# The forward transform of a graph layer's convolution, on two halves of TensorE's rows

## The chip, the cores and the metric

The kernel runs on one core of a Trainium2 chip, in float32. The metric is the time of one launch on the device in microseconds (us); smaller is better.

## What is computed

For 32 graphs of 512 nodes with 256 channels: a layer norm and a relu give `h`; then a layer with a convolution branch, a message branch and a gated update (GRU) is added to `x`. The part that the change touches is in the convolution branch:

```python
h = relu(layernorm(x))
xc = transpose(h, (0, 2, 1))
t = relu(bn1(conv1d(xc, conv1_w, pad=0)))       # 256 -> 256 channels, 1 tap
t = bn2(conv1d(t, conv2_w, pad=8))              # 256 -> 256 channels, 17 taps
x_conv = transpose(relu(t + xc), (0, 2, 1))
# message branch: A = exp(-dist(s, s)) * adj;  x_nmp = A @ relu(h @ w_msg.T + b_msg)
# GRU of [x_conv, x_nmp] and h;  out = x + GRU
```

## The kernel before

The convolution with 17 taps is done in frequencies. The 512 tokens of an image are cut into `W` = 8 pieces of `V` = 64 tokens; each piece, padded to `L` = 80, is transformed by a product with a constant matrix (`fwd`) of 64 rows and 80 columns. The frequencies are multiplied with the transformed weights (`product`, tile py), and brought back later (`inverse`, L585).

The images run in two groups of `GB` = 16. For each group `first_part` goes through the images in a written order (`tc.manual_schedule`): for image b the statistics of image b+2 (VectorE), the transpose of image b+1 (`transpose_h`, tile phT, TensorE, then VectorE into hT), the normalisation of b+2 (VectorE, tile xn), `conv1(b)` (16 records of TensorE in tile pc, then an addition on VectorE and a relu on ScalarE into h), and `windows_to_freq(b - 1, xf)`, the step that is changed. The order of the last calls is: `conv1` of the last image, the transform of the image before it, `by_chunks` (ScalarE copies into hq), the transform of the last image, `by_chunks` of the group's first image. The next step, `message` (tile pm), reads hq.

Between these steps other work is put in through `between(b)`. In the first group it is `weights_to_freq` (L256, tile pw): four products of 17 rows each, on rows 0, 32, 64 and 96, into four banks, which ScalarE and VectorE copy to wst. One such step comes before the transform and one or two after it. In the second group it is `combine_weights` (L886): three loads of GRU weights on the queue of SP, one after the other, and additions on GpSimd and copies on ScalarE, in the same queues as the square root for the layer norm (rstd, L291) and the loads of x.

`windows_to_freq` takes H1, the h of one image, as a tile of 128 tokens by 4 chunks by 256 channels. A chunk holds two pieces of 64 tokens. Before, one product handles both pieces at once: the stationary operand is 128 tokens by 128 channels, and `fwd` is block diagonal, 128 rows by 160 columns, so half of it is zeros. Two chunks go into one bank (320 columns used), and ScalarE copies the bank into xf, whose order is channel, frequency, window. An image takes 2 channel halves x 2 banks x 2 chunks = 8 products and 4 copies.

All banks of PSUM (8) come from one pool, `bank(name)`, and are used in turn; an instruction that needs a bank waits for the reader of the one that had it before. In the profile a float32 product leaves two weight loads and two matmul records; a transpose leaves one.

## Time and profile before

| | |
|---|---|
| median of 8 runs | 1845.65 us (1843.18 to 1849.98) |
| the profiled execution: its own time | 1847.65 us |
| the profiled execution: span from first to last instruction | 1845.9 us |
| mean granted TensorE clock | 0.996 |
| TensorE busy | 1824.3 us (99%) |
| VectorE / ScalarE / GpSimd busy | 1106.7 / 582.4 / 588.4 us |
| first group, first part (30 to 160 us): TensorE busy 130.0 of 130 us, DMA share | 0.93 |
| second group, first part (480 to 578 us): TensorE busy 96.52 of 98 us, DMA share | 0.67 |
| tile px: matmul records, busy, median of one | 512, 77.5 us, 299 ns |
| tile px: weight loads, median of one | 512, 190 ns |
| tile px: copies by ScalarE, median of one | 128, 439 ns |

How to read it: matmul records overlap, so the time of one (299 ns) is longer than the distance to the next. For what a block costs, take the distance from its first start to the first start of the block behind it, in the timeline. PEld is the loading of stationary operands, PE the products.

### The profile page before, as it was taken

To read this page: it belongs to the slowest core of one execution; us is meant where nothing else is said; L and a number is where in the kernel's file an instruction comes from. 1 tells how busy PE (TensorE), PEld (TensorE's weight loads), DVE (VectorE), ACT (ScalarE), POOL (GpSimd) and SP (SyncE) were. 2 spreads that over 40 slices of the span, in tenths; PEclk is the share of its full clock that TensorE was granted. 3 is DMA by queue.
4 is the path that set the end of the run, shared out by engine and by line. 5 is a ranking of instruction groups with operands and counts; after the bars stand their busy time and mean duration, and the time that the engine had idled before them with its cause. 6 is when DMAs were issued, how large, how long until landed. Compare 5 with 4: busy or idle time off the path is not lost.

```text
span 1845.9 us, 20105 instructions
## 1 busy us (share of the span) xinstructions
PE 1824.3 (99%) x6610; PEld 1088.5 (59%) x6610; DVE 1106.7 (60%) x2220; ACT 582.4 (32%) x1083; POOL 588.4 (32%) x572
## 2 busy tenths in 40 slices
PE   8999999999999999999999999999999999999998
PEld 6777666666988676665545554555455544555443
DVE  6774656554885545545266466655666466645666
ACT  4545444432345333333222221222122221222121
POOL 3331333334432344444421323133222323133221
PEclk9999999999999999999999999999999999999999
DMA  8999888775678887777421443234422442244412
GB/s 226 303 278 240 225 240 241 214 188 182 210 245 207 240 248 232 220 203 257 121 86 35 120 120 104 55 81 120 120 81 40 120 120 90 51 99 120 113 24 52
DMA packets 307452, 289.26 MB, mean 157 GB/s; under 512 B 148028, under 2 KB 237148, under 8 KB 306964
## 3 DMA queue, kind: packets, MB, share of 16 engines
q1 hardware_dynamic: 281300, 224.22, 45.8%
q10 hardware_dynamic: 19024, 38.68, 5.9%
q0 software_dynamic: 7024, 25.07, 4.8%
q8 instruction: 53, 0.87, 0.2%
q14 instruction: 51, 0.42, 0.1%
HBM read 191.50 MB, written 96.40 MB: 156 GB/s over the span
## 4 chain that ended last, share of the span: by engine, by line
PE 88%; DMA 4%; DVE 3%; issue 2%; POOL 1%; ACT 1%; SPq 0%; POOLq 0%; ACTq 0%; DVEq 0%
PE pg L597 29%; PE pn L597 14%; PE pn L489 11%; PE py L393 10%; PE pm L439 6%; PE pc L585 5%; PE pc L328 4%; PE px L343 3%; PE pw L256 2%; PE pd L474 2%; DMA w<-in_w_ihT_dram 1%; PE phT L312 1%; DMA hT<-hd 1%; DMA yd<-y 1%; PE psr L463 1%
## 5 line engine op out<-in xcount | busy, mean ns | idle before, releaser
L489 PE MATMUL pn<-A,msg 128*128 128x512 f32 x512 | 225.6, 593 | 0.8 <-DVE A L480 0.8
L597 PE MATMUL pg<-hp,sw 128*128 128x512 f32 x434 | 221.8, 593 | 0.7 <-DVE rz L616 0.5
L597 PE MATMUL pg<-np,sw 128*128 128x512 f32 x434 | 221.6, 592 | 0.0
L597 PE MATMUL pg<-cp,sw 128*128 128x512 f32 x434 | 221.6, 592 | 0.0
L575 POOL TENSOR_TENSOR hp<-hp 128x512 f32<-128x512 f32 x64 | 81.3, 1280 | 412.3 <-DMA hp<-hd 263.6
L372 POOL TENSOR_TENSOR both<-xf 128x256 f32<-128x256 f32 x78 | 60.4, 774 | 322.8 <-PE py L393 291.2
L489 PEld LDWEIGHTS pn<-A,msg 128*128 128x128 f32 x512 | 96.9, 190 | 110.9 <-issue 105.6
L575 POOL TENSOR_TENSOR cp<-cp 128x512 f32<-128x512 f32 x64 | 80.4, 1267 | 230.0 <-ACT cp L591 228.8
L393 PE MATMUL py<-wt,both 128*128 128x256 f32 x624 | 150.5, 384 | 0.7 <-issue 0.7
L612 ACT ACTIVATE rz<-rz,brz 128x512 f32<-128x512 f32 x93 | 67.0, 721 | 260.2 <-DVE rz L616 260.2
L400 DVE TENSOR_TENSOR y<-y,py 128x256 f32<-128x256 f32 x78 | 31.8, 408 | 189.8 <-ACT y L399 189.8
L597 PEld LDWEIGHTS pg<-hp,sw 128*128 128x128 f32 x434 | 82.2, 190 | 104.7 <-issue 97.8
L597 PEld LDWEIGHTS pg<-np,sw 128*128 128x128 f32 x434 | 82.5, 190 | 103.8 <-issue 103.8
L597 PEld LDWEIGHTS pg<-cp,sw 128*128 128x128 f32 x434 | 82.5, 190 | 103.8 <-issue 103.8
L393 PEld LDWEIGHTS py<-wt,both 128*128 128x128 f32 x624 | 114.1, 190 | 43.1 <-issue 27.6
L480 DVE TENSOR_TENSOR A<-e,at 128x512 f32<-128x512 f32 x128 | 114.8, 935 | 37.4 <-ACT e L477 37.2
L359 POOL TENSOR_TENSOR wsum<-wt 128x512 f32<-128x512 f32 x78 | 108.8, 1396 | 55.1 <-DMA wt<-wd 46.2
L735 ACT ACTIVATE nt<-nt,vech 128x512 f32<-128x512 f32 x64 | 46.2, 722 | 235.8 <-DVE nt L734 235.8
L328 PE MATMUL pc<-w,hT 128*128 128x256 f32 x512 | 118.3, 385 | 2.0 <-DVE hT L316 2.0
L439 PE MATMUL pm<-wmsg,hq 128*128 128x259 f32 x512 | 117.4, 382 | 0.2 <-ACT sl L460 0.2
L597 PE MATMUL pn<-cp,sw 128*128 128x512 f32 x224 | 114.4, 592 | 0.0
L597 PE MATMUL pn<-np,sw 128*128 128x512 f32 x224 | 114.4, 592 | 0.0
(146 smaller groups left out, 2959.6 us busy)
## 6 DMA issues: line engine op xcount, KB each, us to landing
wt<-wd SPq DMA_DIRECT2D x160, 256.0 KB, 4.2
adj<-in_adj_dram SPq DMA_DIRECT2D x128, 256.0 KB, 5.3
wd<-wst SPq DMA_DIRECT2D x64, 320.0 KB, 5.4
yd<-y ACTq DMA_DIRECT2D x80, 256.0 KB, 4.0
yt<-yd SPq DMA_DIRECT2D x30, 640.0 KB, 7.3
hd<-hT SPq DMA_DIRECT2D x32, 512.0 KB, 4.4
nd<-nmp ACTq DMA_DIRECT2D x32, 512.0 KB, 4.1
xb<-in_x_dram SPq DMA_DIRECT2D x128, 128.0 KB, 3.7
```

The costliest lines, as they stand in the source:

```text
L328: nc.tensor.matmul(p[:, j, :], HT[b][:, ic, c * P : (c + 1) * P], w1[:, ic, :], start=(ic == 0), stop=(ic == DC - 1))
L343: nc.tensor.matmul(p[:, j * 2 * L : (j + 1) * 2 * L], H1[b][:, c0 + j, ic * P : (ic + 1) * P], fwd, start=True, stop=True)
L359: nc.gpsimd.tensor_tensor(t, WT[g, u][:, 0], WT[g, u][:, 1], op=ALU.add)
L372: nc.gpsimd.tensor_tensor(both[:, 0], re, im, op=ALU.add)
L393: nc.tensor.matmul(dst, v[:, ic, :], w[:, ic, :], start=(ic == 0), stop=(ic == DC - 1))
L439: nc.tensor.matmul(p[:, : D + NS], hq[:, ic, c * P : (c + 1) * P], wmsg[:, ic, :], start=(ic == 0), stop=(ic == DC - 1))
L480: nc.vector.tensor_mul(A[b][:, mc, :], e, at)
L489: nc.tensor.matmul(p, MSG[b][:, mc, dc * P : (dc + 1) * P], A[b][:, mc, :], start=(mc == 0), stop=(mc == NC - 1))
L575: nc.gpsimd.tensor_tensor(t[:, dst, :], t[:, a, :], t[:, b, :], op=sub)
L585: nc.tensor.matmul(bk[:, t0:t1], YT[p][j][:, c, oc * P : (oc + 1) * P], back[:, n : n + t1 - t0], start=(c == 0), stop=(c == len(spans) - ...
L597: nc.tensor.matmul(bk[:, t], sw[:, k, q, o, :], terms[k][q][:, t], start=(first and i == 0), stop=(i == len(ks) - 1), skip_group_check=True)
L612: nc.scalar.activation(rz[:, g, j, :], src, AF.Sigmoid, bias=brz[:, g : g + 1], scale=1.0)
```

## The change

One product per piece instead of one per chunk. `fwd` becomes 128 rows by 80 columns, the same 64 rows of the matrix twice. A chunk's even piece (tokens 0 to 63) is multiplied by rows 0 to 63 of `fwd`, its odd piece (tokens 64 to 127) by rows 64 to 127, each with a stationary operand of 64 rows and 128 columns. Even pieces go into one bank, odd ones into another; a bank takes all four chunks of an image (320 columns used). The products alternate between the two banks. ScalarE copies the two banks after all eight products of a channel half, each to every second window of xf. An image now takes 2 channel halves x 4 chunks x 2 pieces = 16 products and, as before, 4 copies of 320 columns.

```diff
-    forward = np.zeros((2 * V, 2 * L))
-    forward[:V, :L] = forward[V:, L:] = spectrum[:V]
+    forward = np.concatenate([spectrum[:V]] * 2)
...
-    fwd = early.tile([P, 2 * L], FP, name="fwd")
+    fwd = early.tile([P, L], FP, name="fwd")
...
     def windows_to_freq(b, xf):
         w0 = (b % GB) * W
-        per = 2
         for ic in range(DC):
-            for c0 in range(0, NC, per):
-                p = bank(f"px_{b}_{ic}_{c0}")
-                for j in range(per):
-                    nc.tensor.matmul(p[:, j * 2 * L : (j + 1) * 2 * L], H1[b][:, c0 + j, ic * P : (ic + 1) * P],
-                                     fwd, start=True, stop=True)
-                w = w0 + 2 * c0
-                nc.scalar.copy(xf[:, ic, :, w : w + 2 * per],
-                               p[:, : per * 2 * L].rearrange("p (w f) -> p f w", f=L))
+
+            ps = [bank(f"px_{b}_{ic}_{k}") for k in range(2)]
+            for c in range(NC):
+                for k, p in enumerate(ps):
+                    rows = slice(V * k, V * (k + 1))
+                    nc.tensor.matmul(p[:, c * L : (c + 1) * L], H1[b][rows, c, ic * P : (ic + 1) * P],
+                                     fwd[rows, :], start=True, stop=True)
+            for k, p in enumerate(ps):
+                nc.scalar.copy(xf[:, ic, :, w0 + k : w0 + W : 2],
+                               p[:, : NC * L].rearrange("p (w f) -> p f w", f=L))
         del H1[b]
```

## The prediction

> **What bounds the kernel now.** First the page's busy shares, then the groups of TensorE by shape, for the size of what is changed:

> ```profile
> PE 1824.3 (99%) x6610; PEld 1088.5 (59%) x6610; DVE 1106.7 (60%) x2220; ACT 582.4 (32%) x1083; POOL 588.4 (32%) x572
> ```

> ```profile
> L343 PE MATMUL px<-fwd,h 128*128 128x160 f32 x512 | 77.5, 306 | 0.0
> ```

> TensorE is busy all the time, and the step that is changed (tile px) has 77.5 us of it: 32 calls of `windows_to_freq`, each 16 records (a float32 product leaves two, so 8 products). A busy TensorE may still be standing in a queue, though, so next I read the blocks of TensorE in order of time, in the two stages that hold these calls. A middle image of the first group:

> ```profile
> 106.05 2.44 PE L343 MATMUL px<-fwd,h 128*128 128x160 f32 x16
> 108.42 1.88 PE L256 MATMUL pw<-w2p,taps 17*80 17x512 f32 x8
> 110.23 1.09 PE L312 MATMUL phT<-ident,xn 128*128 128x128 f32 x8
> 111.16 3.62 PE L328 MATMUL pc<-w,hT 128*128 128x256 f32 x16
> 114.71 1.10 PE L256 MATMUL pw<-w2p,taps 17*80 17x512 f32 x8
> ```

> Start to next start, the first pw block after a pc takes 1.03 us (114.71 to px at 115.74), but the pw block after px takes 1.81 (108.42 to 110.23). The other engines show why:

> ```profile
> 107.64 1.53 ACT L266 COPY wst<-pw 80x512 f32<-80x512 f32 x3
> 109.22 0.21 PEld L256 LDWEIGHTS pw<-w2p,taps 17*80 17x80 f32 x2 [0.27 <-ACT wst L266]
> 109.58 1.44 DVE L264 COPY wst<-pw 80x512 f32<-80x512 f32 x2 [1.93 <-PE pw L256]
> ```

> The pw block behind px waits for banks that ScalarE empties, and ScalarE started on them late, after the relu of h, which follows VectorE's adds, which follow VectorE's statistics, which follow VectorE's copies of the last pw. That ring (VectorE copies, statistics, hT, xn, h; ScalarE h, copies of pw; the pw block; VectorE copies) does not contain px. In twelve middle images the excess of the pw block is 0.18 to 0.84 us, 0.58 on average. In the second group there is no pw; there I read blocks and then the chain that ended last:

> ```profile
> 532.54 2.34 PE L343 MATMUL px<-fwd,h 128*128 128x160 f32 x16
> 534.71 1.04 PE L312 MATMUL phT<-ident,xn 128*128 128x128 f32 x8
> 535.59 3.62 PE L328 MATMUL pc<-w,hT 128*128 128x256 f32 x16
> 539.04 2.34 PE L343 MATMUL px<-fwd,h 128*128 128x160 f32 x16
> ...
> 545.54 2.34 PE L343 MATMUL px<-fwd,h 128*128 128x160 f32 x16
> 549.29 1.72 PE L312 MATMUL phT<-ident,xn 128*128 128x128 f32 x8 [1.41 <-DVE xn L304]
> ```

> ```profile
> 482.95 7.06 DMA w<-in_w_hhT_dram
> ...
> 507.49 9.29 DMA w<-in_w_ihT_dram
> ...
> 536.72 8.34 DMA w<-in_w_ihT_dram
> ```

> From 480 to 549 us the chain runs through three weight loads for `combine_weights`, GpSimd's additions behind them and VectorE's steps, not through TensorE, which stands still 1.41 us at 549.29 for it. Only after that are TensorE's blocks the chain.

> **The change part by part.** *The products.* Before, a px call lasts 2.17 us start to start (532.54 to 534.71), so a record of 160 columns costs 2.17/16 = 0.136. After, a call has 32 records of 80 columns, 16 on each half of the rows. Do halves run side by side, and what limits one half? The trace has no 64-row product; the nearest row is pd, four products on rows 0, 32, 64 and 96:

> ```profile
> 311.00 0.31 PEld L474 LDWEIGHTS pd<-sr,sl 9*128 9x128 f32 x8 [0.34 <-issue]
> ```

> Eight weight loads of 128 columns, 0.183 each by the tile's view, fill 0.31 us: four begin together, and the next four about 0.11 later. So loads on different rows overlap, and one set of rows takes one load per 0.107 (0.31 less 0.183, less the 0.02 in which the four begin). Streaming 80 columns costs less: records of 512 and 256 columns come every 0.43 (pn, last stage) and 0.216 (3.45/16 in pc), so 0.83 ns a column, 0.07 for 80. The load is the limit: 16 rounds of 0.108, the last without a following load: 15 x 0.108 + 0.08 = 1.70. A call saves 2.17 - 1.70 = 0.47. Bounds: streaming alone would limit (16 x 0.07 = 1.1, saving 1.07), or loads of both halves in series (32 x 0.107 + 0.07 = 3.49, costing 1.32). I take 1.70, since pd is the closest row.

> *Going over to half rows and back.* The trace has this between 128 rows and 17 or 9 rows. A pc block lasts 3.55 before pw (111.16 to 114.71) but 3.45 before px: 0.09 to enter. The pw block's two rounds of 0.43 make 0.86 of its 1.03; about 0.07 of the rest is its first, smaller load, 0.10 leaving. px between pw and pw lasts 2.37, not 2.17: 0.09 for the next entry, 0.11 for first weights that nothing hides. phT behind pw takes 0.93, not 0.87: 0.06. So half-row px costs, from pc and into phT, 0.09 + 0.11 + 0.10 + 0.06 = 0.36, into pc or pm 0.41; bounds 0, if halves need no such step, and about double. In the second group a call therefore nets 0.47 - 0.36 = 0.11. In the first group most px calls already stand between two pw, and the step is paid now. [...]

> *Copies.* Four per call as before, each 128x320 (434 to 442 ns); two now come free together after each half of the call. Their output steps by two elements instead of running over four neighbours; no row shows that for ScalarE. A copy at half the speed would still end before phT needs its bank in the first group (the first px copy ends about 0.65 us before the phT block), and ScalarE sits idle for 52.9 us waiting for h in the second; I take 0, bound 2.5 us (eight copies ahead of hq, 0.3 each). *The constant* fwd halves in size and loads at the start under w1: 0.

> *What arrives at the end.* First group: the first call is followed by 1.6 us of waiting: 0. Twelve middle calls are outside the ring: 0 (bound 0.47 each, 5.6). The call at 154.28, whose pw blocks wait for nothing now: 0.47 less some waiting for px copies, 0.3. The two joint calls at 162.09 (4.35 to pm): 31 x 0.108 + 0.08 + 0.41 = 3.84, saving 0.51; but pm reads hq, which ScalarE copies until then:

> ```profile
> 164.81 1.17 ACT L425 COPY hq<-hT 128x512 f32<-128x512 f32 x2
> ```

> so pm can't start before some 166.03 instead of 166.44: 0.41. Second group: eleven calls up to 549: 0, the loads set the end (bound 0.11 each). Calls at 554.39 and 560.90: 0.11 each; at 567.40, into pc: 0.06; the joint calls at 573.03 by the same limit (hq until 576.92): 0.40. Sum: 0.3 + 0.41 + 0.22 + 0.06 + 0.40 = 1.4 us. The profiled execution took 1847.65 with a span of 1845.9, 2.0 over the median of 1845.65. So its own time would be 1846.3, and the median 1844.2.

> **The rivals.** *The loads of the two halves go in series* (slower). A block of 128 tokens then takes 4 x 0.107 = 0.43 instead of 0.27, a call 1.32 more. First group: twelve calls with 0.58 of cover, (1.32 - 0.58) x 12 = 9; the last three calls 3 x 1.32 + 0.41 = 4.4. Second group: eleven x 1.68 less about 2 of present waits = 16.5; afterwards 3 x 1.68 + 3.05 = 8. Together 38: 1883.7. It decides from about 0.27 us a block on: there the steps between row modes alone (14 x 0.36 + 0.41 - 2) make 3.5 us. Against it: the eight pd loads in 0.31 us. For it: no product of 64 rows was seen, and none kept two halves going over 16 rounds.

> *The waits follow TensorE after all* (faster): the ring and the load chain begin earlier because TensorE does. Then 12 x 0.47 + 11 x 0.11 = 6.8 more, 1837.4. For it: VectorE waits 1.93 us for the pw block, so the ring has a TensorE part. Against it: that part waits for ScalarE.

> **How the numbers follow.** A measurement of this kernel can tell about 0.2%, 3.7 us, from no change. My forecast, 1844.2, has 0.56 (own range 1841 to 1848); 0.50 of it within 0.2%, 0.04 faster, 0.02 slower. The faster rival has 0.24, 0.20 of it past the line; serial or partly serial loads 0.20, 0.18 past it. Faster 0.24, same 0.56, slower 0.20. The range takes in the faster rival and loads that overlap in part, and leaves out full series: 1837.4 to 1852.

> **What would show it.** px: 1024 records; a lone call of the second group 1.70 + 0.11 + 0.10 = 1.9 us from px start to phT start, and the pc before it 3.55 instead of 3.45; a middle image of the first group with px at 1.9 too and a pw block behind it longer by what px lost; that image's period unchanged (9.57 us from phT at 110.23 to phT at 119.80 now). The stillness at 549 us grows or starts sooner. Wrong it would be if px calls take over 2.2 us (series), or if the first group's period shrinks by 0.4.

## The result and the profile after

The kernel after takes 1853.59 us (median of 15 runs, 1849.13 to 1862.66), the kernel before 1846.28 beside it (42 runs): ratio 1.0038, 95% interval 1.0029 to 1.0047. The change costs some 7 us, where 1.4 us less were forecast; the measured median also lies above the range. Two causes make up the loss: in the first group the granted clock of TensorE falls (0.95 from 35 to 165 us in the profile, before 1.00), because a half-row call uses half as many cells of the array (1.07 us of the whole array instead of 2.13, an estimate below); in the second, a call issues twice the instructions (32 records instead of 16), and fetches of TensorE's code fall into the two weight loads that set the end (10.41 and 8.72 us, before 9.29 and 8.34).

The parts of the change did what was said of them. First the page's busy shares, then the group of px by shape:

```profile
PE 1826.4 (99%) x7122; PEld 1083.1 (59%) x7122; DVE 1108.5 (60%) x2220; ACT 582.4 (32%) x1083; POOL 589.1 (32%) x572
```

```profile
L343 PE MATMUL px<-fwd,h 64*128 64x80 f32 x1024 | 66.8, 277 | 0.5 <-DVE h L330 0.5
```

512 records more, 10.7 us less of px than the 77.5 before, and yet TensorE as a whole is busy 2.1 us longer. What else got longer stands in the timeline of TensorE, over two middle images of the first group (start, length, records):

```profile
105.29 1.43 PE L343 MATMUL px<-fwd,h 64*128 64x80 f32 x18
106.87 1.11 PE L343 MATMUL px<-fwd,h 64*128 64x80 f32 x14 [0.15 <-DVE h L330]
107.92 2.13 PE L255 MATMUL pw<-w2p,taps 17*80 17x512 f32 x8
109.98 1.72 PE L311 MATMUL phT<-ident,xn 128*128 128x128 f32 x8
111.50 4.71 PE L327 MATMUL pc<-w,hT 128*128 128x256 f32 x16
116.14 1.10 PE L255 MATMUL pw<-w2p,taps 17*80 17x512 f32 x8
117.17 2.02 PE L343 MATMUL px<-fwd,h 64*128 64x80 f32 x32
119.12 1.10 PE L255 MATMUL pw<-w2p,taps 17*80 17x512 f32 x8
120.15 1.09 PE L311 MATMUL phT<-ident,xn 128*128 128x128 f32 x8
```

The pc block, untouched by the change, takes 4.64 us to the next start (111.50 to 116.14) where it took 3.55; phT takes 1.51 instead of 0.93. The granted clock says why. In the windows view (from and to, length, then busy time with records of TensorE, weight loads, VectorE, ScalarE and GpSimd, then the granted clock, the share of the DMA engines and GB/s), first before, then after:

```profile
35.00:165.00 130.00, 130.00 (x776) 94.23 (x775) 97.20 (x252) 69.97 (x157) 39.54 (x60) 1.00 0.93 281
```

```profile
35.00:165.00 130.00, 129.44 (x955) 92.09 (x954) 95.13 (x242) 67.01 (x149) 39.15 (x60) 0.95 0.89 267
...
106.90:110.30 3.40, 3.40 (x25) 1.98 (x26) 1.41 (x3) 3.40 (x9) 0.00 (x0) 1.00 0.89 293
110.30:113.70 3.40, 3.40 (x14) 2.95 (x12) 3.37 (x12) 0.89 (x2) 0.97 (x1) 0.50 0.91 266
```

For 3.4 us TensorE runs at half speed, after 3.4 us in which it was "busy" for all of 3.40. Over 35 to 165 us the clock is 0.95; before it was 1.00 there. The half-clock stretches of 3.4 us begin at 89.8, 110.3, 130.8 and 151.2 us, besides 6.8 us from 28.4 on; before had two up to 165 us, at 12.6 and 29.6, and none in the middle images. The page's own clock row shows 9 in every slice in both kernels, since a slice is 46 us. From the px at 84.73 to the px at 157.92 seven images take 73.19 us; before, from 85.94 to 154.28, 68.34.

The profiled execution of the kernel after (own time 1847.78 us) is the shortest of its sixteen, with a mean clock of 0.992; the others have 0.987 to 0.992 (median 0.991), those of before a median of 0.996. The longest, 1862.66, has 0.987. In the traces of before and after every stretch of the clock is at 1.00 or 0.50; if that holds in the other runs too, 0.996 is 15 us at half speed and 0.991 is 33 us, 18 us more, which is up to 9 us of TensorE's work (an estimate). Run by run the time follows the clock: a straight line through the 16 runs of the kernel after, and another through the 108 runs of before that were taken beside all experiments, both fall by 2.0 us for each 0.001 of clock. By that the 0.005 between the medians are some 10 us (an estimate), so the clock alone is large enough for the whole loss; what the code fetch adds to the time has to be read from pairs of kernels, below.

The second group, in the timeline and in the chain that ended last:

```profile
529.07 2.02 PE L343 MATMUL px<-fwd,h 64*128 64x80 f32 x32
531.02 1.10 PE L311 MATMUL phT<-ident,xn 128*128 128x128 f32 x8
...
551.12 1.72 PE L311 MATMUL phT<-ident,xn 128*128 128x128 f32 x8 [0.75 <-DVE xn L303]
```

```profile
507.75 10.41 DMA w<-in_w_ihT_dram
...
538.17 8.72 DMA w<-in_w_ihT_dram
```

A lone call is 1.945 us (529.07 to 531.02), as predicted. But the two loads on the chain, 9.29 and 8.34 us before, are 1.12 and 0.38 longer, and phT comes at 551.12 instead of 549.29 (the first px of this group began 0.24 us later than in before).

### The profile page after: what moved, and what is told of

The parts are those of the page before. It is cut to its first block, busy times and chain, and to the rows that moved or that the text cites. A ratio compares the mean times of both kernels' runs of the same rounds, so it can differ in the third digit from the quotient of the medians.

```text
span 1846.0 us, 21126 instructions
## 1 busy us (share of the span) xinstructions
PE 1826.4 (99%) x7122; PEld 1083.1 (59%) x7122; DVE 1108.5 (60%) x2220; ACT 582.4 (32%) x1083; POOL 589.1 (32%) x572
## 4 chain that ended last, share of the span: by engine, by line
PE 84%; DVE 2%; issue 2%; DMA 2%; POOL 1%; SPq 0%; ACT 0%; POOLq 0%; DVEq 0%; ACTq 0%
PE pg L597 29%; PE pn L597 14%; PE pn L489 12%; PE py L393 11%; PE pm L439 6%; PE pc L585 5%; PE pd L474 2%; PE pc L327 2%; DMA w<-in_w_ihT_dram 1%; PE px L343 1%; PE psr L463 1%; PE phT L311 1%; DVE stats L284 0%; DVE xn L303 0%; PE pw L255 0%
## 5 line engine op out<-in xcount | busy, mean ns | idle before, releaser
L597 PEld LDWEIGHTS pg<-hp,sw 128*128 128x128 f32 x434 | 82.2, 190 | 104.8 <-issue 97.1
L327 PE MATMUL pc<-w,hT 128*128 128x256 f32 x512 | 123.2, 396 | 1.6 <-DVE hT L315 1.6
L597 PE MATMUL pn<-hp,sw 128*128 128x512 f32 x224 | 114.4, 592 | 0.0
```

The source lines that it names most:

```text
L327: nc.tensor.matmul(p[:, j, :], HT[b][:, ic, c * P : (c + 1) * P], w1[:, ic, :], start=(ic == 0), stop=(ic == DC - 1))
L597: nc.tensor.matmul(bk[:, t], sw[:, k, q, o, :], terms[k][q][:, t], start=(first and i == 0), stop=(i == len(ks) - 1), skip_group_check=True)
```

## The experiments

The theory formed from the two profiles was that dips of the clock in the first group make the loss, by one of two reasons: too few cells of the array in use, or TensorE's waiting and the dearer steps between row modes. All ratios are to the kernel before, run beside it, with 95% intervals.

**Which group loses.** e1 and e2 keep both forms of the step and choose by the image:

```diff
+    def windows_to_freq(b, xf):
+        (by_halves if b >= GB else by_chunks_of_two)(b, xf)      # e1; e2: b < GB
```

> Half rows in the second group of images only, full rows in the first. The theory that I form from the two traces: what is lost is lost in the first group, where the granted clock falls to one half for stretches of 3.4 us (five times between 28 and 155 us after the change, three times in the whole launch before it, each costing about 1.7 us). It expects the first group's times of before, a mean clock of 0.995 to 0.997, and 1845 to 1846 us beside 1846.3 of before (1.1 us saved by the late calls of the second group). The rival, that going over to half rows costs more than I priced wherever it happens, expects about half of the loss here, 1849 to 1850.

> Half rows in the first group only, full rows in the second. The theory of the clock in the first group expects the whole loss, 1852 to 1855 us with a mean clock of 0.989 to 0.991. The rival of a dear step between row modes expects 1849 to 1850, since most calls of the first group stand between two pw and paid that step before the change.

e2: 1.0031 (1.0020 to 1.0041), median clock 0.992, half-clock stretches at the same places as in the kernel after. e1: 1.0020 (1.0008 to 1.0031), and this was the surprise: not a gain of 1 us, but a loss. Its first group was as before; in the second TensorE got ahead, stood still longer before the step at 549 (1.78 us before phT, 1.41 in before), and a stretch of half clock followed:

```profile
549.20:552.60 3.40, 1.55 (x15) 1.04 (x13) 2.08 (x5) 0.27 (x1) 3.01 (x4) 1.00 0.64 235
552.60:556.00 3.40, 3.40 (x12) 2.85 (x12) 3.37 (x13) 2.72 (x7) 0.27 (x1) 0.50 0.39 154
```

Its w_ihT loads took 10.67 and 8.85 us. With half rows in the first group alone (e2) the first load took 9.3. So both groups lose: the first by the clock, the second by longer loads, and by the clock too (one stretch, at 552.6 us in e1 and at 523.3 in the kernel after).

**What lowers the clock: cells or waiting?** Between the first and the last change of the clock in the traces of before and after, changes lie a whole multiple of 3.41 us apart. For every such stretch of 3.41 us I added, over TensorE's records, streaming time x rows/128 x columns/128, as a share of the stretch (an estimate from the trace: 0.83 ns a column, since records of 512 columns start every 0.43 us; 128 rows by 128 columns, the largest shape in the trace, stand for the whole array). A full-row px call gives 2.13 us of the whole array, a half-row call 32 x 0.067 x 0.5 = 1.07, a pw step 0.28. The stretches ahead of half clock had 0.24 to 0.32 in the kernel after (from 35 us on); in before no stretch in the middle images had under 0.38. e3 raises the sum of px and pw without touching their order or banks (the added columns are not read):

```diff
-                    nc.tensor.matmul(p[:, c * L : (c + 1) * L], H1[b][rows, c, ic * P : (ic + 1) * P],
+                    nc.tensor.matmul(p[:, c * P : (c + 1) * P], H1[b][rows, c, ic * P : (ic + 1) * P],
...
-            nc.tensor.matmul(p[:ROWS, :], taps[32 * q : 32 * q + KT, :],
+            nc.tensor.matmul(p, taps[32 * q : 32 * q + KT, :],
```

(`fwd` and `taps` are 128 columns wide there.)

> The changed kernel with more of TensorE's array in use in the same order and nearly the same time: each half-row px product streams 128 columns instead of 80 (a repeat of the first 48, not read; its weight load takes as long as that anyway), and each pw product has 128 stationary columns instead of 80 (a repeat, not read). Two theories of why the clock falls. Cells: what counts is rows x columns in use x time in a window of 3.4 us; by my sum over the profiled runs every window under 0.375 of the array was followed by half clock and none above. It expects the halved stretches of the first group to go nearly all, clock 0.994 to 0.996, 1844 to 1848 us. Waiting: what counts is that TensorE stands and waits behind ScalarE longer than before; the waits are not touched here, so it expects 1852 to 1855 us and 0.989 to 0.991 as in the changed kernel.

1.0015 (1.0000 to 1.0029), clock 0.994, one stretch left between 35 and 165 us. In the first group the clock did what cells said. The time (1850.26) stayed above the 1844 to 1848 expected, and the median clock below the 0.996 of before; in the profile the second group's loss is still there (load 10.20 us, half clock from 555.5 and from 593.0 us).

e6 takes cells away from the kernel before and leaves its order and banks; the odd pieces are left out:

```diff
-                    nc.tensor.matmul(p[:, ...], H1[b][:, c0 + j, ic * P : (ic + 1) * P], fwd, ...)
+                    nc.tensor.matmul(p[:, ...], H1[b][:V, c0 + j, ic * P : (ic + 1) * P], fwd[:V], ...)
```

> The kernel before, but each px product takes only rows 0 to 63 (the stationary tile and fwd are cut to 64 rows; 160 columns, banks, order and copies as before). The odd pieces are left out, so their windows come out zero. Cells theory (the clock falls when the cells of the array in use, streaming time x rows/128 x columns/128, are under about 0.375 of a 3.4 us window): px falls from 2.13 to 1.07 us of full array per call, as in the kernel after, though neither the banks nor the order of the products changed; so half-clock stretches appear in the first group (3 to 6 of them between 80 and 160 us), the clock is 0.990 to 0.993 and the time 1850 to 1855. Waiting theory (the stretches come from the two banks filled together and TensorE waiting for conv1's banks): as before, no more than 1 half-clock stretch between 35 and 165 us, clock 0.996 and 1845 to 1849 (a step into half rows was there for pw already; in the second group 0.36 per call is hidden up to 549 us, some 1.5 us are not).

1.0056 (1.0043 to 1.0069), median clock 0.993: the rows alone bring it down (before 0.996), with px as long as before (2.37 us between pw blocks) and no two banks. But its profile has 10.2 us of half clock from 29.6 on and one stretch at 152.5, not the 3 to 6 expected between 80 and 160. First px to first pm is 142.5 us (before 137.4), and 99.6 (before 97.3) in the second group; of its loss of some 10 us the remaining 3 stay unexplained.

e10 and e11 decide it. In the kernel after, both fill the wait behind px with two products that stream equally long; one uses 1.7% of the cells, the other all:

```diff
+            if ic == 1 and b < GB:
+                for i in range(2):
+                    nc.tensor.matmul(ps[1][:16, 320:], fwd[:17, :16], H1[b][:17, i, : 6 * 32], ...)   # e10
+                    nc.tensor.matmul(ps[1][:128, 320:], ident, H1[b][:128, i, : 6 * 32], ...)         # e11
```

> The kernel after, and behind the px products of each image of the first group two products that nobody reads: 17 rows by 16 columns, 192 columns streamed (four records of 0.16 us, 0.64 us in all), into unused columns of the last px bank. They fill TensorE's wait for the pw banks behind px with work that uses 1.7% of the array's cells. If cells set the clock: the half-clock stretches stay as in the kernel after (4 to 6 between 35 and 165 us), clock 0.988 to 0.992, first pm at 169.5 to 172 us, time 1852 to 1857. If it is TensorE's waiting that sets it: no more than 1 stretch there, clock 0.994 to 0.996, time 1846 to 1850, and the same in e11.

> The same as e10 in place, count and streaming time, but the two products take 128 rows by 128 columns (ident against h), so all cells of the array for 0.64 us, 0.19 of a 3.4 us window. The lowest windows of the kernel after (0.24 to 0.33) come to 0.43 and more, over the 0.375 to 0.38 at which stretches ended so far. If cells set the clock: no more than 1 half-clock stretch between 35 and 165 us, clock 0.993 to 0.996, first pm at 167 to 169.5 although TensorE has 15 x 0.64 us more to do, time 1847 to 1851: less than e10. If waiting sets it: as e10, or dearer by the step into and out of 128 rows (15 x 0.2 to 0.4 us, part of it hidden).

The windows of e10 and then of e11:

```profile
35.00:165.00 130.00, 129.70 (x940) 91.72 (x939) 93.94 (x246) 63.40 (x138) 39.79 (x60) 0.91 0.89 254
```

```profile
35.00:165.00 130.00, 129.75 (x1011) 93.90 (x1008) 96.00 (x251) 67.92 (x149) 39.51 (x60) 0.99 0.92 271
```

TensorE is busy for 129.7 us in both; one is granted 0.91, the other 0.99, with no new stretch between 35 and 165. A busy record can hide a wait (in before a pw block that waits for ScalarE is busy for 1.88 us, one that waits for nothing 1.10), so count also the share of the full-clock stretches in which any product streams, whatever its cells (an estimate from the trace): 0.83 in e10, 0.84 in e11, in e6 0.92 as in before. The waits are alike, the cells and the clock are not. So here it is cells. e10 has seven stretches of 3.4 us between 35 and 165 us, one of them begun before, and its first pm comes at 180.5 us, still later than expected. The times were 1.0066 (1.0049 to 1.0084) and 1.0048 (1.0034 to 1.0063): with overlapping intervals, e11's gain in time isn't shown. It is 3 us slower than expected and its first pm starts at 173.5 (expected 167 to 169.5), because in it TensorE itself sets the image: pc 3.55, pw 1.03, px with filler 3.28, pw 1.22, phT 0.93, together 10.0 us without a wait.

**The longer load of the second group.** Issues and bytes around the load are the same in before and e1; but one packet of 16 KB is different. The queue view over the load, before (507.5 to 516.8 us) and then e1 (508.0 to 518.7):

```profile
q14 instruction: 1, 0.01, 0.2%
...
w<-in_w_ihT_dram SPq DMA_DIRECT2D x1, 768.0 KB, 9.3
```

```profile
q8 instruction: 1, 0.02, 0.6%
q14 instruction: 1, 0.01, 0.2%
...
w<-in_w_ihT_dram SPq DMA_DIRECT2D x1, 768.0 KB, 10.7
```

Queue q8, which the profile calls instruction, fetches 53 such packets in before and 57 in after:

```profile
q8 instruction: 57, 0.93, 0.2%
```

Four more, 64 KB, for 256 more products: 256 B each (an estimate), and e1 and e2, with 128 more, fetch 55 each. So I take it for TensorE's code; it comes every 16 us or so in the second group instead of every 22. In e1 a fetch began 2.85 us after the load's issue and took 0.96 us; the load took 1.4 us longer than in before. e7 moves all of TensorE's code by 7.25 KB (29 x 256 B, by the same estimate), by products of one column at the start of the program, and changes nothing else of e1; e8 moves before's code so that a fetch falls into its load:

```diff
         transpose_h(b0)
+        if g == 0:
+            p = bank("pad")
+            for i in range(29):          # e7, on e1; e8: 33, on the kernel before
+                nc.tensor.matmul(p[:1, i : i + 1], ident[:, :1], ident[:, :1], start=True, stop=True)
         fill()
```

> e1 (half rows in the second group alone) with 29 products of one column at the start of the program, in a stretch where TensorE waits 1.67 us; they move all of TensorE's later code by 29 x 256 B = 7.25 KB. Code-fetch theory (a 16 KB fetch of TensorE's code, 0.95 us long, falls at 510.9 into the w_ihT load of 508.0 to 518.7 and makes one DMA engine late by as much; a half-row px issues twice the instructions, so fetches come every 15.4 us instead of 21.8): the fetches come some 7 us earlier against the work, about 503.9, 519.5 and 537.3, outside both loads; the load takes 9.3 us instead of 10.67, the second one about 8.4 instead of 8.85, and the first part of the second group ends 1.3 to 1.8 us sooner against its start. Time 1847 to 1849 (the clock's stretch at 552 stays). If the longer load comes from something else (the x loads or hd stores beside it, other places in memory), it stays at 10.4 to 10.7 and the time at 1849 to 1851.

> The kernel before with 33 products of one column at the start, in the same waiting stretch: TensorE's later code moves by 8.25 KB and no other work changes. Code-fetch theory: the fetches at 501.7, 522.9 and 544.9 come about 11 us earlier, at 490.7, 511.8 and 533.8; one falls into the w_ihT load (507.5 to 516.8), which takes 10.4 to 10.7 us instead of 9.29, with full-row px; the first part of the second group ends about 1.2 us later against its start, and the time is 1847.5 to 1849.5. If the half-row px itself lengthens the load: 9.3 us, and the time within 1 us of the kernel before.

That the fetch makes one DMA engine late was my estimate: no view shows it, only the length of the load. The first load in the chain that ended last, in e1 and then in e7:

```profile
508.05 10.67 DMA w<-in_w_ihT_dram
```

```profile
506.56 9.45 DMA w<-in_w_ihT_dram
```

The second load took 7.86, first px to pm in the second group 97.38 us (e1 99.68, before 97.26), and the whole 1.0007 (0.9996 to 1.0018). In e8 the fetch came at 511.8 as expected and the load took 9.95, 0.66 more than before but less than expected; first px to pm took 98.16 us, and in the whole time, 1.0003 (0.9990 to 1.0016), it can't be seen. In seventeen kernels' profiles the first load takes 10.2 to 10.7 us where a fetch begins within the first 3.2 us after its issue (after, e1, e3, e4, e12), 9.95 with a fetch after 6.1 us (e8), and 9.3 to 9.5 in all others, whatever px looks like. The second load goes the same way: in the kernel after a fetch at 544.2 us falls into it too.

**Is that all?** e14 moves the code of the kernel after by the same 29 products; e13 adds e3's wider products to that.

> The kernel after with the 29 small products of e7 at the start, which move TensorE's later code by 7.25 KB so that no fetch of it falls into the w_ihT loads. Two causes theory (clock in the first group, code fetch in the second): w_ihT load 9.3 to 9.5 us instead of 10.41, the second group's first part about 1 us shorter from its first px to pm (97.1 to 97.5 us; 98.14 in the kernel after), the clock stays at 0.989 to 0.992, and the ratio to before falls from 1.0038 by 0.0005 to 0.0013: 1.0025 to 1.0033, 1849.5 to 1851.5. If the fetch is worth nothing in this kernel: 1.0035 to 1.0045.

> Both remedies on the kernel after, with half rows everywhere: e3's wider px and pw products (more cells, not read) and the 29 small products. Two causes theory: nothing is left of the loss: from e3's 1.0015 less 0.0013 (what the moved code gave in e7 against e1) comes 1.0000 to 1.0005, 1846 to 1848, clock 0.994 to 0.996, w_ihT load 9.3 to 9.5 us. If a third cause is at work: 1.0012 and more.

e14: 1.0021 (1.0006 to 1.0035), clock 0.991, load 9.28, 97.02 us from px to pm in the second group (98.14 in the kernel after). e13: 0.9990 (0.9978 to 1.0001), clock 0.9965, load 9.28, and in its windows:

```profile
35.00:165.00 130.00, 130.00 (x1008) 94.69 (x1008) 97.94 (x253) 70.22 (x156) 39.55 (x60) 1.00 0.94 284
```

With both remedies nothing is left of the loss, even slightly less than expected; no third cause is needed. Four pairs differ by the 29 products alone: the kernel after and e14, e1 and e7, e3 and e13, e12 and e15 (below). The ratio falls by 0.17, 0.13, 0.25 and 0.16%. In each pair the intervals overlap, and e13 also has the better clock (0.9965, e3 0.994), but all four go the same way, while in e8, where a fetch was moved into the load, 33 such products gained nothing.

**Could half rows gain anything?** The prediction said that a ring of VectorE and ScalarE sets the first group's images. e4 cuts it in the kernel after, e5 in the kernel before: from the third image on, the relu of h is issued behind ScalarE's copies of pw.

```diff
-            nc.scalar.activation(h1, h1, AF.Relu)
+            if not late:
+                nc.scalar.activation(h1, h1, AF.Relu)
...
+            late = g == 0 and b > b0 + 1
...
             for step in one:
                 step()
+            if late:
+                relu(b)
```

> The changed kernel, and in the first group, from the third image on, ScalarE's two relu of h are issued after its copies of the first pw step instead of before them, so that those copies don't stand behind a relu that waits for VectorE. The ring that I read in the profile of before (VectorE adds, ScalarE relu, copies of pw, second pw step) is cut. If px is outside the ring and inside TensorE's own order, the period of a middle image falls from about 9.6 us to 0.93 + 3.55 + 1.03 + 1.95 + 1.03 = 8.5, some 12 us in all: 1834 to 1840 us; windows of 3.4 us then hold over 0.4 of the array and little clock is lost by either theory. If the second pw step waits for something else (VectorE's copy), the time stays at 1850 or above.

> The kernel before with one edit, the later relu of e4: in the first group, from the third image on, ScalarE's relu of h is issued behind its copies of pw. If the ring (and not px) set the image's period, and the half-row px is what costs the clock: the first group's image falls from 9.57 to about 8.9 us, the first pm starts at about 158 to 159 us instead of 166.4, the granted clock stays near 0.996, and with the second group unchanged (w_ihT load 9.3 us, first pm of group 2 some 411 us after the first pm of group 1) the time is 1837 to 1840, below e4's 1842.5. If the half-row px was a gain once the ring is cut (12 calls x 0.24 us and more in the first group, 0.11 each in the second), this kernel is slower than e4: 1843 to 1847.

e4: 0.9970 (0.9960 to 0.9981), e5: 0.9969 (0.9956 to 0.9983), a shorter kernel both times, e4 (1842.52; expected 1834 to 1840) by less than expected. In e5 an image has no wait left and takes 8.91 us instead of 9.57:

```profile
104.68 1.09 PE L312 MATMUL phT<-ident,xn 128*128 128x128 f32 x8
...
113.59 1.09 PE L312 MATMUL phT<-ident,xn 128*128 128x128 f32 x8
```

The first pm starts at 158.77 (before 166.44). That e5 would beat e4 by some 4 us is not shown: its median is 1838.83, but e4 ran beside other runs of before, and the two ratios are level. Three more look for what half rows add: e9 is e5 with half rows in the last two calls of each group only (`b % GB >= GB - 2`); e12 is e4 with e3's wider products; e15 is e12 with the moved code.

> e5 (full rows, later relu) with half-row px in the last two calls of each group alone, of which the last three are followed by nothing that waits for another engine. The joint calls take 3.73 us instead of 4.35; in the first group some 0.4 of it arrives (pm reads hq), in the second 0.6; the step behind pc costs 0.1 each. Sum -0.8 us against e5 (ratio 0.9969): ratio 0.996 to 0.997, time 1836.5 to 1840, clock as e5's. If a half-row call draws a half-clock stretch even here, or the 4 x 2 KB more of code move a fetch into the loads of the second group (9.3 us to 10.5), it is 1840 to 1843.

> e4 (half rows everywhere, later relu) with the px products 128 columns wide and pw's stationary tile 128 columns, as in e3 (the added columns are not read). If cells set the clock and the half rows lose by it alone: the stretches left in e4 (150 and 543 us) go, clock 0.995 to 0.997 against e4's 0.9935, px still shorter than with full rows (about 1.95 against 2.37 us between pw blocks), time 1838 to 1841, level with e5 (1838.8) or 1 to 2 us above it, since the code fetch still lengthens the load of the second group. If the clock isn't it: as e4, ratio 0.997 and clock 0.9935, or longer by the wider products.

> e12 (half rows, later relu, more cells) with the 29 small products: does half-row px gain anything when the ring, the clock and the fetch are all out of the way? Against e5 (full rows, later relu, 0.9969) its px calls are 0.22 to 0.4 us shorter; if they set the end wherever no load does, the ratio is 0.9960 to 0.9966; if TensorE's time is still not what sets the end, 0.9968 to 0.9972. w_ihT load 9.3 to 9.5 us, clock 0.995 to 0.997.

e9: 0.9971 (0.9954 to 0.9989); first px to pm is 0.74 us shorter than in e5 in the first group and 0.51 in the second (worked out: 0.4 and 0.6, less 0.1 a group), too little to be seen in the whole. e12: 0.9978 (0.9964 to 0.9992), load 10.7; the median clock rises to 0.9955 (e4 0.994), but a stretch at 545.2 us stays. e15: 0.9962 (0.9948 to 0.9975), the lowest ratio, but its interval holds e5's. Cutting the ring is worth 0.3%; half rows on top of it are not told apart from nothing.

## Why the prediction was wrong

- **The price of the call was right.** Predicted 1.9 us from px to phT, measured 1.945; pc before it 3.55, measured 3.549; the joint calls 3.84, measured 3.73. Loads of the two halves run side by side, a pair every 0.112 us (predicted 0.108), so the rival of loads in series fell. After the step at 549, the predicted 0.22 + 0.06 + 0.40 = 0.68 us came in: phT to pm took 27.38 us (551.12 to 578.50) against 28.08.
- **The step that failed first is "Twelve middle calls are outside the ring: 0 (bound 0.47 each, 5.6)".** The ring was there (e4, e5), and while the clock was full it held the period as predicted: the four images from 47.46 us on took 37.27 us, in before (from 48.76 us on) 37.18. But the term bounded only what a shorter px could give. It held the other blocks at their durations, that is the clock at before's 0.996, and had no term for a loss. The cover it counted on, 0.58 us of waiting per image, became part of what lowered the clock: the stretches of 3.4 us ahead of half clock, with pw, waiting and px of half the cells, hold 0.24 to 0.32 of the array by the sum above, where none of before's middle images held under 0.38. The seven images from 84.73 us on, with four half-clock stretches, cost 4.85 us more in the profile, and e2 puts the first group's share at 0.31%, 5.7 us.
- **The second is "eleven calls up to 549: 0, the loads set the end (bound 0.11 each)".** The loads did set the end, but their lengths were taken as fixed. With twice the instructions in px there were more fetches of code (57 instead of 53), and one fell into each load (at 509.7 and 544.2 us): +1.1 and +0.4 us in the kernel after. e14 against the kernel after puts it at 0.17% with intervals that overlap, e7 against e1 at 0.13%.
- **"The stillness at 549 grows or starts sooner"** held in e1 (px to phT was 2.5 us longer than a lone call, in before 1.57) and not in the kernel after (0.8), where a half-clock pc at 524 held TensorE back.
- **The range** went up to 1852 by way of loads that overlap in part. It contained neither mechanism, and the median came out 1.6 us above it.
- **The waits of before gave no hint of it.** In its middle images and the second group no wait of TensorE was longer than 1.6 us, by the lengths of its blocks, and the clock there was full. In the kernel after, even a stretch with 3.40 us of 3.40 busy (106.90 to 110.30) was followed by half clock.

## What to carry to other kernels

Here a px call with half the rows in each product became 1.12 times as fast (2.17 to 1.945 us), where its streaming alone would have been halved (2.13 to 1.07, an estimate), since pairs of weight loads set its pace (one every 0.112 us); and the granted clock of the first group fell from 1.00 to 0.95. So before cutting a product down, add up rows x columns x time in the 3.4 us around it, above all where TensorE waits beside it. Splitting the products added four code fetches here, and where one fell early into a load on the chain, the load took 10.2 to 10.7 us instead of 9.3: look where the fetches fall. When a part is outside the ring, cut the ring (0.3% here) instead of the part.
